# Three layers of edge convolution: comparison keys kept twice instead of four times, a fourth buffer for the compared keys, and count products in turns of three

## The chip, the cores and the metric

The kernel runs on one core of a Trainium2 chip. The metric is the device time of one execution in microseconds; three runs of the kernel before lie between 518.28 and 518.4 us. All times below are microseconds unless marked ns.

The engines are named as the profile names them: PE is TensorE (its matmuls), PEld the weight loads of TensorE, DVE VectorE, ACT ScalarE, POOL GpSimd, and SP the engine that issues most transfers.

## The reference

There are N = 2500 nodes with 256 features, and 80000 edges from `src` to `dst`, sorted by `dst`. A layer norm and a relu give h. Then come three layers and a final product over the concatenated results:

```python
def _edge_conv(x, src, dst, W, b):
    xi = x[dst]
    xj = x[src]
    m = jnp.concatenate([xi, xj - xi], axis=-1) @ W + b
    s = jax.ops.segment_sum(m, dst, num_segments=N)
    cnt = jax.ops.segment_sum(jnp.ones((dst.shape[0],), m.dtype), dst, num_segments=N)
    return s / jnp.maximum(cnt, 1.0)[:, None]

xs, h = [x], x                       # x: the normalized input
for W, b in ((W0, b0), (W1, b1), (W2, b2)):
    h = jax.nn.relu(_edge_conv(h, src, dst, W, b))
    xs.append(h)
return jnp.concatenate(xs, axis=-1) @ Wf + bf     # and the input is added
```

A layer is linear in the gathered features, so it can be done with a matrix A of counts: A[m, n] is how many edges go from node m to node n. Summing over edges then is a product with A, and the degrees are its column sums.

## The kernel before, in words

**Numbers.** Nodes are padded to NT = 20 tiles of 128. Six destination nodes (W = 6) make a window; there are 417 windows. For each window the kernel keeps a list of up to 256 edges (CH = 2 chunks of 128). Columns of A are worked in five groups (`GWS`: 84, 84, 84, 84 and 81 windows, that is 504 or 486 destination nodes).

**Keys.** For each edge there are two small numbers: the source node within its tile (0 to 127) in `key_m`, and tile and destination place (0 to 119) in `key_n`. `key_copy` (ACT, lines 579 to 584) writes them as bf16, each value four times in a row.

**Compare (DVE).** `compare(b)` (lines 753 to 767) takes four windows (BW = 4, eight chunks of 128 edges) and makes one-hot rows by two comparisons with running numbers: `one_m` (8 x 128 values) and `one_n` (8 x 120 values). The stored repeat makes the innermost piece of the key operand four adjacent values; the next step of that operand has stride 0, so the same four are read again for the whole row. The buffers of both are as many as `AHEAD`, 3.

**Count (PE).** `counts(b)` (lines 771 to 778) multiplies `one_m` by `one_n`, two bf16 products for each of the four windows, eight per call, into one PSUM bank. In the profile this is `bank<-one_n,one_m`.

**Take (ACT).** `take_counts(b, a)` casts a bank into the columns of the tile `a`, which holds A for one group. In the profile this is `a<-bank`.

**Aggregate (PE).** `layer(l, g, a, own)` (lines 816 to 838) adds up, over 20 tiles of source nodes, four products a tile: features in a high and a low part, `zh` and `zl`, times `a` (`pa<-a,zh` and `pa<-a,zl`). Four more units of work are the product with the node's own features (`pa<-hT,wt`); `own` says where in the sequence of 24 units they stand. It ends with a relu into `hT` on ACT.

**Stages.** The first 62 us prepare: edge lists are found, x is normalized, the first node products are made (`pz`), and the first group of A is counted. Their order over all engines is written out by hand in the string `order` (lines 863 to 872): Bn is `compare(n)`, Cn `counts(n)`, En `take_counts(n)`, and 21 calls of `compare` belong to a group. Then comes layer 0 (lines 899 to 927), group by group: while a group is aggregated, the next group's A is counted in between. `build` (lines 786 to 797) yields after each **turn**: two calls of `counts`, two of `take_counts`, two of `compare(c + AHEAD)`. The 21 calls of a group make 11 turns, the last with one call, and `at` (line 907) spreads them over the 24 units; the last stands after unit 22, with one unit to follow. All four engines keep to the program order in this stage (the class `InOrder`). `degrees` and `by_count` run beside it: the first makes the node degrees, with two small products (`bank<-ident_b,deg_b`), the second multiplies `hT` by them on DVE.

Layers 1 and 2 load finished groups of A back from HBM and count nothing. The banks for counts, degrees and node products are four in this stage (pool `ps`).

Of the kernel before, what the change touches and what calls it, by code (L numbers as in the profile page):

```python
# [11 lines left out]
OP = mybir.AluOpType  # L12
# [254 lines left out]
BF16 = mybir.dt.bfloat16  # L267
# [19 lines left out]
def run(it):  # L287
    for _ in it:
        pass
# [16 lines left out]
def chain(*its):  # L306
    for it in its:
        yield from it
# [3 lines left out]
def by_windows(ctx: ExitStack, tc: tile.TileContext, x, src, dst, Ws, bs, Wf, bf, out, missing):  # L312
# [3 lines left out]
    P = 128  # L316
# [9 lines left out]
    CH = 2  # L326
    S = 8
    CAP = CH * P
    NW = (N + W - 1) // W
# [1 line left out]
    WG = (NW + P - 1) // P  # L331
    NB = NT * W
    BW = 4
    AHEAD = 3
    GWS = []
    while sum(GWS) < NW:
        GWS.append(min(84, NW - sum(GWS)))
# [13 lines left out]
    const = ctx.enter_context(tc.tile_pool(name="const", bufs=1))  # L351
# [9 lines left out]
    def bank():  # L361
        return ps[-1].tile([P, 512], F32, name="bank")
# [3 lines left out]
    hT = const.tile([P, DC, NP], F32, name="hT")  # L366
    zh = const.tile([P, NT, D], F32R, name="zh")
    zl = const.tile([P, NT, D], F32R, name="zl")
    key_m = const.tile([P, NW, CH, 4], BF16, name="key_m")
    key_n = const.tile([P, NW, CH, 4], BF16, name="key_n")  # L370
    away = const.tile([P, WG, CAP], BF16, name="away")
    cnt = const.tile([P, NP], BF16, name="cnt")
    share = const.tile([P, NT], F32, name="share")
# [40 lines left out]
    ws = [None] * L  # L414
# [164 lines left out]
    def key_copy(i, q):  # L579
        n = min(P, NW - i * P)  # L580
        to = (key_m, key_n)[q]
        ACTo.copy(to[:, i * P:i * P + n, :, :].rearrange("p n j r -> p j n r"),
                  parts[i][:, q * CAP:(q + 1) * CAP].rearrange("p (j n) -> p j n", j=CH)[:, :, :n]
                  .unsqueeze(3).to_broadcast([P, CH, n, 4]))

    def degrees(i):

# [20 lines left out]
    def shares():  # L608
        cnt_n = bank()
        for t in range(NT):  # L610
            PEo.matmul(cnt_n[:, t:t + 1], cnt[0:1, t * P:(t + 1) * P], ones_b, start=True, stop=True)
        found = hot.tile([P, 1], F32, name="found")
        DVEo.reduce_sum(found, deg.rearrange("p i c -> p (i c)"), axis=mybir.AxisListType.X)
        pf = bank()
        PEo.matmul(pf[0:1, 0:1], found, ones, start=True, stop=True)
        DVEo.tensor_scalar(missing, pf[0:1, 0:1], float(E), None, op0=OP.not_equal)
        yield
        some = hot.tile([P, NT], F32, name="some")
        DVEo.tensor_scalar(share, cnt_n[:, :NT], 1.0, None, op0=OP.max)
        DVEo.reciprocal(share, share)  # L620
        DVEo.tensor_scalar(some, cnt_n[:, :NT], 1.0, None, op0=OP.min)
        DVEo.tensor_mul(share, share, some)
        yield
# [123 lines left out]
    def new_a(g):  # L747
        return apools[g % 2].tile([P, NT, GS], F32R, name="a")

    windows = [(g, s, min(BW, GWS[g] - s)) for g in range(NG) for s in range(0, GWS[g], BW)]  # L750
    ones_of = {}

    def compare(b):
        if b >= len(windows):
            return
        g, s, nb = windows[b]
        w0 = sum(GWS[:g]) + s
        one_m = hot.tile([P, BW * CH, P], BF16, name="one_m", bufs=AHEAD)
        one_n = hot.tile([P, BW * CH, NB], BF16, name="one_n", bufs=AHEAD)
        k = nb * CH  # L760
        for one, iota, keys_, m in ((one_m, iota_m, key_m, P), (one_n, iota_n, key_n, NB)):
            DVEo.tensor_tensor(
                one[:, :k, :].rearrange("p k (m r) -> p k m r", r=4),
                iota.rearrange("p (m r) -> p m r", r=4).unsqueeze(1).to_broadcast([P, k, m // 4, 4]),
                keys_[:, w0:w0 + nb, :, :].rearrange("p w j r -> p (w j) r").unsqueeze(2)
                .to_broadcast([P, k, m // 4, 4]), op=OP.is_equal)
        ones_of[b] = one_m, one_n

    counted = {}
# [1 line left out]
    def counts(b):  # L771
        _, s, nb = windows[b]
        one_m, one_n = ones_of.pop(b)
        pb = counted[b] = bank()
        for w in range(nb):
            for j in range(CH):
                PEo.matmul(pb[:, w * NB:(w + 1) * NB], one_m[:, w * CH + j, :], one_n[:, w * CH + j, :],
                           start=(j == 0), stop=(j == CH - 1))

    def take_counts(b, a):  # L780
        _, s, nb = windows[b]
        ACTo.copy(
            a[:, :, s * W:(s + nb) * W].rearrange("p t (w c) -> p t w c", c=W),
            counted.pop(b)[:, :nb * NB].rearrange("p (w t c) -> p t w c", w=nb, c=W))

    def build(g, a):

        bs = [b for b in range(len(windows)) if windows[b][0] == g]
        for b in bs[::2]:
            two = [b, b + 1] if b + 1 in bs else [b]  # L790
            for c in two:
                counts(c)
            for c in two:
                take_counts(c, a)
            for c in two:
                compare(c + AHEAD)
            yield

    def finish(g, a):
        c0, n = group_of(g)  # L800
        POOLo.tensor_copy(a[PAD:PAD + 1, NT - 1, :n], cnt[PAD:PAD + 1, c0:c0 + n])
        SP.dma_start(a_dram[g][:, :, :n], a[:, :, :n].bitcast(F32))
        yield
# [7 lines left out]
    def by_count(g):  # L811
        c0, n = group_of(g)
        for o in range(DC):
            DVEo.tensor_mul(hT[:, o, c0:c0 + n], hT[:, o, c0:c0 + n], cnt[:, c0:c0 + n])

    def layer(l, g, a, own, PE=PE, ACT=ACT):

        c0, n = group_of(g)
        pa = ps_agg.tile([P, DC, 512], F32, name="pa")
        ways = [(o, c) for o in range(DC) for c in range(DC)]  # L820
        units = [(0, k) for k in range(NT)]
        for i, u in enumerate(own):
            units.insert(u + i, (1, i))
        last = {}
        for kind, i in units:
            last.update({o: (kind, i, o) for o in (range(DC) if kind == 0 else ways[i][:1])})
        for kind, i in units:
            if kind == 0:
                for o in range(DC):
                    for z in (zh, zl):  # L830
                        PE.matmul(pa[:, o, :n], z[:, i, o * P:(o + 1) * P], a[:, i, :n],  # L831
                                  start=(i == 0 and z is zh), stop=(z is zl and last[o] == (kind, i, o)))
            else:
                o, c = ways[i]
                PE.matmul(pa[:, o, :n], ws[l][0][:, c, o * P:(o + 1) * P], hT[:, c, c0:c0 + n],  # L835
                          start=False, stop=(last[o] == (kind, i, o)))
            yield
        ACT.activation(hT[:, :, c0:c0 + n], pa[:, :, :n], AF.Relu)  # L838
# [8 lines left out]
    a = new_a(0)  # L847
# [4 lines left out]
        "se": lambda i: search(*((0, 1), (1, WG))[i]), "ge": get_edges,  # L852
        "ka": key_parts, "km": key_low, "kb": key_high, "kt": key_turn,
        "k1": lambda i: key_copy(i, 0), "k2": lambda i: key_copy(i, 1),
        "io": small_numbers, "ws": lambda: DVEo.tensor_sub(ws[0][0], ws[0][0], ws[0][1]),
        "st": stats, "rs": lambda g: spread(*groups[g]), "sq": lambda g: roots(*groups[g]),
# [11 lines left out]
        k11 N8 L6 B4 E2 L5 C3 B5 C4 T8 E3 E4 C5 V9 R8 E5 ge3 ka2 H9 sc2 Z7 H7 F8 G7 B6 N3 N2 ka3 km2 T2 R2 km3  # L868
        kb2 C6 T3 kb3 B7 L7 kt2 Z2 B8 B9 L9 E6 C7 k22 k12 kt3 H2 N4 E7 B10 k13 k23 Z8 L2 C8 T4 C9 E8 C10 H8 E9
        F9 B11 B12 C11 G8 E10 C12 R4 E12 E11 B13 F5 B14 C13 R3 B15 C14 E13 E14 L8 B16 Z3 G9 B17 C15 C16 H3 E15  # L870
        G5 B18 F3 C17 E16 C18 F4 E17 B19 C19 Z4 L3 G3 B20 E18 C20 B21 F2 E19 B22 E20 H4 L4 G4 B23 G2 ws
    """

    def perform(order):
# [24 lines left out]
    for g in range(NG):  # L899
        at = {}  # L900
        own = LATE
        if g + 1 < NG:
            a1 = new_a(g + 1)
            one = build(g + 1, a1)
            left = (len([b for b in windows if b[0] == g + 1]) + 1) // 2
            units = NT + DC * DC
            at = {(i + 1) * (units - 1) // left - 1 for i in range(left)}
            if g:
                own = [u + 1 - i for i, u in enumerate(sorted(at)[1:8:2])]
        else:  # L910
            extra = shares()
        for u, _ in enumerate(layer(0, g, a, own, PEo, ACTo)):
            if u in at:
                next(one)
            next(extra, None)
            if g == 0 and u % 2:
                next(extra, None)
            if g == 0 and u == NT // 2 + 3:
                by_count(0)
            if u == NT - 1 and g + 1 < NG:  # L920
                run(extra)
                by_count(g + 1)
        run(extra)
        if g + 1 < NG:
            run(finish(g + 1, a1))
            held, a = a, a1
        extra = chain(degrees(g + 2) if g + 2 < WG else ())
# [71 lines left out]
```

## Time and profile before

| | |
|---|---|
| median of three runs | 518.34 us (518.28 to 518.4) |
| the profiled execution | 518.31 us, of which the profiled span is 516.4 |
| PE busy | 509.2 us, 99% of the span |
| PEld busy | 405.9 us, 79% |
| DVE busy | 213.9 us, 41% |
| ACT busy | 138.4 us, 27% |
| granted PE clock | 0.999 |
| preparation | 0 to 61.7 us |
| layer 0, with four groups of A counted beside it | 61.7 to 211 us |

Busy time is added up per engine. A matmul's end is modelled and consecutive matmuls overlap, so a busy PE need not be a PE at full rate. What one matmul costs its successor is read from the difference of two starts in the timeline.

### The profile page before, as it was taken

What the parts mean: (1) busy time and instruction counts of PE and PEld (TensorE: products, weight loads), DVE (VectorE), ACT (ScalarE), POOL (GpSimd) and SP (SyncE); (2) the same over time, 40 slices, a digit from 0 to 9 for tenths busy, and PEclk for the clock granted to TensorE, in tenths of its full rate; (3) what the DMA queues carried; (4) which work ended last, traced back from release to release, by engine and by line L of the source; (5) the groups of instructions that cost most, each with busy time, mean ns of one, the idle gap of its engine ahead of it and who ended that gap; (6) DMA issues with size and microseconds to landing.
All of it is one profiled execution on the core that took longest, in us unless ns stands there. A gap on an engine that the chain in (4) does not pass through costs nothing.

```text
span 516.4 us, 6986 instructions
## 1 busy us (share of the span) xinstructions
PE 509.2 (99%) x2864; PEld 405.9 (79%) x2864; DVE 213.9 (41%) x455; ACT 138.4 (27%) x307; POOL 70.1 (14%) x103
## 2 busy tenths in 40 slices
PE   8999999999999999999999999999999999999996
PEld 4898888677777788788787878787887878787875
DVE  7999889887988840360101010103501010101033
ACT  5777576654643320330000000004300000000000
POOL 2680000000000000017242414200000000000000
PEclk9999999999999999999999999999999999999999
DMA  9110008950906428011576665100005564740023
GB/s 277 50 43 0 1 2 321 340 215 13 378 12 224 178 86 311 22 30 48 176 265 207 235 232 210 32 1 1 1 0 202 199 225 176 242 144 20 1 84 121
DMA packets 38111, 68.74 MB, mean 133 GB/s; under 512 B 1200, under 2 KB 37064, under 8 KB 38070
## 3 DMA queue, kind: packets, MB, share of 16 engines
q1 hardware_dynamic: 35798, 63.49, 34.9%
q0 software_dynamic: 1344, 3.61, 2.3%
q10 hardware_dynamic: 928, 1.11, 0.7%
q8 instruction: 24, 0.39, 0.3%
q14 instruction: 17, 0.14, 0.1%
HBM read 40.03 MB, written 28.18 MB: 132 GB/s over the span
## 4 chain that ended last, share of the span: by engine, by line
PE 96%; DMA 2%; DVE 0%; issue 0%; SPq 0%
PE pa L831 35%; PE pa L280 21%; PE bank L732 10%; PE bank L280 10%; PE bank L709 7%; PE pz L280 7%; PE pa L835 6%; DMA wf<-in_L_gnn_Wf_dram 2%; DMA dst_i<-in_dst_dram 1%; PE turned L280 1%; DVE acc L734 0%; DVE first L280 0%; SPq L280 0%
## 5 line engine op out<-in xcount | busy, mean ns | idle before, releaser
L831 PE MATMUL pa<-a,zh 128*128 128x504 f32 (+1 forms) x400 | 156.8, 392 | 0.0
L831 PE MATMUL pa<-a,zl 128*128 128x504 f32 (+1 forms) x400 | 155.0, 387 | 0.0
L734 DVE SCALAR_TENSOR_TENSOR acc<-bank,share,acc 128x256 f32<-128x256 f32 x60 | 29.0, 484 | 214.0 <-PE bank L732 214.0
L831 PEld LDWEIGHTS pa<-a,zl 128*128 128x128 f32 x400 | 75.2, 188 | 15.0
L831 PEld LDWEIGHTS pa<-a,zh 128*128 128x128 f32 x400 | 75.2, 188 | 15.0
L280 PE MATMUL pa<-a,zh 128*128 128x504 f32 (+1 forms) x200 | 84.7, 423 | 0.0
L280 DVE TENSOR_TENSOR one_m<-iota_m,key_m 128x1024 bf16<-128x1024 bf16 (+1 forms) x105 | 72.4, 690 | 15.4 <-PE bank L280 15.2
L280 PE MATMUL pa<-a,zl 128*128 128x504 f32 (+1 forms) x200 | 77.7, 388 | 0.0
L838 ACT ACTIVATE hT<-pa 128x1008 f32<-128x1008 f32 (+1 forms) x10 | 10.1, 1005 | 239.2 <-PE pa L835 239.2
L280 ACT CAST a<-bank 128x480 fp32r<-128x480 f32 (+1 forms) x105 | 54.5, 561 | 65.5 <-PE bank L280 62.7
L280 DVE TENSOR_TENSOR one_n<-iota_n,key_n 128x960 bf16<-128x960 bf16 (+1 forms) x105 | 68.3, 650 | 0.0
L280 PEld LDWEIGHTS <-one_m 128*128 128x128 bf16 x834 | 45.7, 98 | 13.5 <-DVE one_m L280 7.4
L280 PE MATMUL bank<-one_n,one_m 128*128 128x120 bf16 x834 | 53.9, 217 | 0.0
L732 PE MATMUL bank<-wf,hT 128*128 128x256 f32 x240 | 53.6, 379 | 0.0
L732 PEld LDWEIGHTS bank<-wf,hT 128*128 128x128 f32 x240 | 45.6, 190 | 9.9 <-issue 4.1
L280 PEld LDWEIGHTS pa<-a,zh 128*128 128x128 f32 x200 | 37.8, 189 | 9.0 <-issue 2.3
L280 PEld LDWEIGHTS pa<-a,zl 128*128 128x128 f32 x200 | 37.7, 188 | 8.1 <-issue 2.3
L719 DVE SCALAR_TENSOR_TENSOR zl<-bank,share,zh 128x256 fp32r<-128x256 f32 x38 | 18.4, 484 | 55.9 <-ACT zh L718 55.8
L835 PE MATMUL pa<-hT,wt 128*128 128x504 f32 (+1 forms) x80 | 35.2, 583 | 0.0
L709 PE MATMUL bank<-wb,hT 128*128 128x256 f32 x160 | 34.9, 379 | 0.0
L709 PEld LDWEIGHTS bank<-wb,hT 128*128 128x128 f32 x160 | 30.4, 190 | 4.9 <-issue 0.9
L835 PEld LDWEIGHTS pa<-hT,wt 128*128 128x128 f32 x80 | 15.2, 190 | 14.6 <-issue 13.8
(113 smaller groups left out, 337.9 us busy)
## 6 DMA issues: line engine op xcount, KB each, us to landing
a<-a_dram SPq DMA_DIRECT2D x5, 5040.0 KB, 17.3
a_dram<-a SPq DMA_DIRECT2D x4, 5040.0 KB, 17.2
a_dram<-a SPq DMA_DIRECT2D x1, 4860.0 KB, 17.1
a<-a_dram SPq DMA_DIRECT2D x1, 4860.0 KB, 16.6
zf<-in_x_dram POOLq DMA_DIRECT2D x19, 128.0 KB, 3.1
out_dram<-acc SPq DMA_DIRECT2D x19, 128.0 KB, 1.7
wf<-in_L_gnn_Wf_dram SPq DMA_DIRECT2D x4, 256.0 KB, 9.1
acc<-in_x_dram SPq DMA_DIRECT2D x1, 896.0 KB, 10.0
```

Source lines behind the costliest of these rows:

```text
L280: return self.tc.keep_in_program_order(call(*args, **kwargs))
L709: PE.matmul(pz[:, :D], hT[:, c, t * P:(t + 1) * P], ws[l][1][:, c, :], start=(c == 0), stop=(c == DC - 1))
L719: DVE.scalar_tensor_tensor(zl[:, t, :], pz[:, :D], sc, zh[:, t, :].bitcast(F32), op0=OP.mult, op1=OP.subtract)
L732: PE.matmul(po[:, :D], hT[:, c, t * P:(t + 1) * P], wfs[l][:, c, :], start=(c == 0), stop=(c == DC - 1))
L734: DVE.scalar_tensor_tensor(acc[:, t, :], po[:, :D], share[:, t:t + 1], acc[:, t, :], op0=OP.mult, op1=OP.add)
L831: PE.matmul(pa[:, o, :n], z[:, i, o * P:(o + 1) * P], a[:, i, :n], start=(i == 0 and z is zh), stop=(z is zl and last[o] == (kind, i, o)))
L835: PE.matmul(pa[:, o, :n], ws[l][0][:, c, o * P:(o + 1) * P], hT[:, c, c0:c0 + n], start=False, stop=(last[o] == (kind, i, o)))
L838: ACT.activation(hT[:, :, c0:c0 + n], pa[:, :, :n], AF.Relu)
```

## The change

The repeat of the keys goes from four to two (`REP`), which halves `key_m` and `key_n`; the comparisons read two adjacent values again and again instead of four. `AHEAD` goes from 3 to 4, so `one_m` and `one_n` have four buffers each, and `compare` runs one call further ahead; `B24` joins the written order. A turn of `build` has three calls instead of two (`TURN`): 21 calls make 7 turns. The turns stand after the units 2, 5, 8, 12, 15, 18 and 22 (before: 1, 3, 5 and so on to 19, and 22), and the four own units of groups 1 to 4 follow the turns after the old units 5, 8, 12 and 15.

```diff
@@ -331,7 +331,9 @@
     BW = 4
-    AHEAD = 3
+    TURN = 3
+    REP = 2
+    AHEAD = 4
@@ -366,8 +368,8 @@
-    key_m = const.tile([P, NW, CH, 4], BF16, name="key_m")
-    key_n = const.tile([P, NW, CH, 4], BF16, name="key_n")
+    key_m = const.tile([P, NW, CH, REP], BF16, name="key_m")
+    key_n = const.tile([P, NW, CH, REP], BF16, name="key_n")
@@ -581,7 +583,7 @@
         to = (key_m, key_n)[q]
         ACTo.copy(to[:, i * P:i * P + n, :, :].rearrange("p n j r -> p j n r"),
                   parts[i][:, q * CAP:(q + 1) * CAP].rearrange("p (j n) -> p j n", j=CH)[:, :, :n]
-                  .unsqueeze(3).to_broadcast([P, CH, n, 4]))
+                  .unsqueeze(3).to_broadcast([P, CH, n, REP]))
@@ -760,10 +762,10 @@
             DVEo.tensor_tensor(
-                one[:, :k, :].rearrange("p k (m r) -> p k m r", r=4),
-                iota.rearrange("p (m r) -> p m r", r=4).unsqueeze(1).to_broadcast([P, k, m // 4, 4]),
+                one[:, :k, :].rearrange("p k (m r) -> p k m r", r=REP),
+                iota.rearrange("p (m r) -> p m r", r=REP).unsqueeze(1).to_broadcast([P, k, m // REP, REP]),
                 keys_[:, w0:w0 + nb, :, :].rearrange("p w j r -> p (w j) r").unsqueeze(2)
-                .to_broadcast([P, k, m // 4, 4]), op=OP.is_equal)
+                .to_broadcast([P, k, m // REP, REP]), op=OP.is_equal)
@@ -786,14 +788,13 @@
         bs = [b for b in range(len(windows)) if windows[b][0] == g]
-        for b in bs[::2]:
-            two = [b, b + 1] if b + 1 in bs else [b]
-            for c in two:
-                counts(c)
-            for c in two:
-                take_counts(c, a)
-            for c in two:
-                compare(c + AHEAD)
+        for i in range(0, len(bs), TURN):
+            for b in bs[i:i + TURN]:
+                counts(b)
+            for b in bs[i:i + TURN]:
+                take_counts(b, a)
+            for b in bs[i:i + TURN]:
+                compare(b + AHEAD)
             yield
@@ -868,7 +869,7 @@
-        G5 B18 F3 C17 E16 C18 F4 E17 B19 C19 Z4 L3 G3 B20 E18 C20 B21 F2 E19 B22 E20 H4 L4 G4 B23 G2 ws
+        G5 B18 F3 C17 E16 C18 F4 E17 B19 C19 Z4 L3 G3 B20 E18 C20 B21 F2 E19 B22 E20 H4 L4 G4 B23 B24 G2 ws
@@ -902,11 +903,11 @@
-            left = (len([b for b in windows if b[0] == g + 1]) + 1) // 2
+            left = -(-len([b for b in windows if b[0] == g + 1]) // TURN)
             units = NT + DC * DC
             at = {(i + 1) * (units - 1) // left - 1 for i in range(left)}
             if g:
-                own = [u + 1 - i for i, u in enumerate(sorted(at)[1:8:2])]
+                own = [u + 1 - i for i, u in enumerate(sorted(at)[1:5])]
```

## The prediction

> **What bounds the kernel now.** I read the page's busy times first, then its slices, then the sums of two stretches, the waits, and last the timeline around one turn.
>
> ```profile
> PE 509.2 (99%) x2864; PEld 405.9 (79%) x2864; DVE 213.9 (41%) x455; ACT 138.4 (27%) x307; POOL 70.1 (14%) x103
> ...
> DVE  7999889887988840360101010103501010101033
> ```
>
> PE is never idle for long, so a gain has to come from fewer PE instructions or from their spacing. The DVE row shows two programs: nearly full to the fourteenth slice (180 us), nearly empty after. The change touches only the full part. The sums of busy time over the preparation from 20 us on and over layer 0 (stretch; PE, PEld, DVE, ACT, POOL; clock) say how full:
>
> ```profile
> 20.00:61.68 41.68, 41.68 (x341) 37.19 (x339) 39.59 (x83) 30.08 (x59) 16.66 (x16) 1.00 0.07 20
> 61.68:190.01 128.33, 128.33 (x1067) 99.13 (x1065) 107.41 (x189) 65.92 (x161) 5.18 (x6) 1.00 0.47 169
> ```
>
> DVE is the second bound: 39.59 of 41.68 us in the preparation, 107.41 of 128.33 in layer 0. The waits say who waits for whom there (total, times, longest):
>
> ```profile
> DVE one_m L280 <- PE bank L280: 15.2, 31, 2.0
> ...
> PEld L280 <- DVE one_m L280: 7.4, 28, 0.3
> ```
>
> The comparisons wait 15.2 us for PE to free buffers, which is their slack. The other line looks like PE waiting for comparisons, but it is a weight load of at most 0.3 us each time, the same length as waits that other turns put down to "issue"; the timeline shows that it delays no matmul:
>
> ```profile
> 83.16 0.39 PE L280 MATMUL pa<-a,zh 128*128 128x504 f32 x1
> 83.16 0.19 PEld L280 LDWEIGHTS pa<-a,zl 128*128 128x128 f32 x1
> ...
> 83.39 0.39 PE L280 MATMUL pa<-a,zl 128*128 128x504 f32 x1
> ...
> 83.62 0.85 PEld L280 LDWEIGHTS <-one_m 128*128 128x128 bf16 x16 [0.27 <-DVE one_m L280]
> 83.62 1.02 PE L280 MATMUL bank<-one_n,one_m 128*128 128x120 bf16 x16
> ...
> 84.42 0.19 PEld L280 LDWEIGHTS pa<-a,zh 128*128 128x128 f32 x1
> 84.45 0.47 PE L280 MATMUL pa<-a,zh 128*128 128x504 f32 x1
> 84.53 0.19 PEld L280 LDWEIGHTS pa<-a,zl 128*128 128x128 f32 x1
> 84.76 0.39 PE L280 MATMUL pa<-a,zl 128*128 128x504 f32 x1
> ```
>
> From start to start: pa to pa 0.23 (83.16 to 83.39), the last pa to the counts also 0.23, sixteen counts 0.83 (0.052 each). But the first pa after the counts takes 0.31 (84.45 to 84.76). Its weight load starts 0.03 before it, while inside a run the load starts a whole matmul ahead. So **each return from counts costs about 0.08 us**. The last turn of group 1, with only eight counts, pays the same: first pa at 125.54, the next at 125.86. So it is a price per turn, not per count. A turn followed by an own unit pays it too: 104.53 to 107.20 is 2.67, against 16 x 0.052 + 2 x 0.424 + 4 x 0.2275 = 2.59.
>
> [...] starts 0.60 and 0.57 apart. [...]
>
> ```profile
> L280 DVE TENSOR_TENSOR one_m<-iota_m,key_m 128x1024 bf16<-128x1024 bf16 x104 | 72.2, 694 | 15.4 <-PE bank L280 15.2
> ...
> L280 DVE TENSOR_TENSOR one_n<-iota_n,key_n 128x960 bf16<-128x960 bf16 x104 | 68.0, 654 | 0.0
> ...
> L280 ACT CAST a<-bank 128x480 fp32r<-128x480 f32 x104 | 54.2, 564 | 63.2 <-PE bank L280 60.4 <-issue 2.8
> ```
>
> **The change part by part.**
>
> 1. *Turns of three.* Four groups are counted beside layer 0: 44 turns become 28. The counts themselves stay. Saved: 16 x 0.083 = **1.33 us**, all on PE, the bounding engine. The written order of PE's instructions confirms 24 counts where 16 stood, and that own units still stand right behind a turn.
>
> 2. *Degree products.* Six small matmuls that stand alone between pa runs cost the same return. Two places change, one to each side; I count **+0.02** for the twelve in group 0, which now follow four pa and not the counts. The degrees are computed on DVE, in group 0 behind the comparisons of the turn after unit 5: these start 0.6 after the turn, last 3 x 1.17 = 3.5, and the degrees 0.6 more, 4.7 together. PE asks for them after 24 counts, 12 pa and 24 counts, 1.25 + 2.82 + 1.25 = 5.3. In groups 1 and 2 an own unit adds 0.85 to that. Covered; without the cover, at most 0.5 us each.
>
> 3. *The last turn of a group.* The next group's first pa needs all columns of its A. Before, the last turn had eight counts: PE then had one unit to do while ACT cast one bank. In the page's time at 93.22: counts start, cast 93.83 to 94.39, pa at 94.45. Now there are 24 counts (1.25 us) and three casts. The first cast starts 0.63 after the counts (83.62, 84.25), two take 1.02, so three end near 0.63 + 1.53 = 2.16, plus some 0.05 to be seen. PE arrives at 1.25 + 0.85 = 2.10 behind group 0 (own unit last) and 1.25 + 0.91 + 0.08 = 2.24 in groups 1 to 3. So a **new wait of about 0.1 us** once, and none to 0.15 at the other three, if the weight load cannot go ahead. I take +0.15 in all, with 0 to 0.6 for the range. Queued behind those casts on ACT is the group's relu into `hT`, needed only by work a unit of layer later; behind the last column on POOL is one row copy and on SP the 17 us store, which must be over before the buffer's next use about 30 us later.
>
> 4. *Banks.* Three count banks and up to two degree banks rotate over four. ACT empties one in 0.51; a turn comes every 4.4 us. A degree product right behind a turn takes the fourth bank, the next the first again, which is cast by 1.2 us after the turn began; its counts last 1.25. Taken as nothing. No run shows a shortage, so up to 0.3 us a group for the range.
>
> 5. *Fourth buffer, B24.* B24 adds 1.17 us to DVE at the end of the preparation, before `ws`, which is needed at unit 20 of group 0, over 20 us later. Its compare needs a buffer that count 20 frees at 60.1. In a turn DVE has 3 x 1.17 = 3.5 us of work in 4.4 and one compared call in stock. Nothing on the path. That the new buffers move the tiles behind them in memory I cost at nothing, as spacing does not show addresses.
>
> 6. *Keys twice.* Six casts of 1.02 us on ACT write half as much; the cast of 512 values into `zh` takes 0.59, so ACT gets some 2.5 us back in the preparation. PE is gapless there and DVE takes its keys well ahead; no gain. The comparisons keep their 1.17 us a pair [...]. I take 0; the bound above is 1.02 more a pair.
>
> Sum: -1.33 + 0.02 + 0.15 = -1.16. From the profiled 518.31, which is 516.4 of span plus 1.9 around it, that gives 517.15; against the median 518.34, as near the same, **517.1 us**.
>
> **Rivals.**
>
> *Slower: the comparisons [...].* [...] Price: call 20 is counted at 59.66 and its comparison ended at 57.84, so the preparation has 1.8 us of slack over 21 calls; 21 x 1.02 - 1.8 = 20 us. In layer 0 a group would need 21 x 2.19 + 1.8 = 48 us of DVE against 31 of PE: some 60 us over the four groups. Time: about **597 us**. The point from which it decides is low: more than 0.09 us a pair (8%) uses up the preparation's slack; above 1.39 a pair DVE bounds layer 0 too.
>
> *No difference: the saving is eaten.* The waits of step 3 reach 0.15 at all four ends, and degree products or banks wait once. For it: ACT's margin there is under 0.1 us by my sum. Against: it needs nearly all the upper ends. Time: 517.4 to 518.3, about **517.8**.
>
> *The saving is not per turn.* If a scheduler split the turns, or if the return cost grew with the counts in front of it, nothing is won: 518.3. The written order excludes the first; eight, sixteen and two counts with the same 0.08 to 0.09 speak against the second.
>
> **How the numbers follow.** What a measurement of this kernel can tell from no change is about 0.2%, 1.04 us, so my forecast stands just beyond that edge. I give the forecast as worked out, up to 517.3, 0.54; the eaten saving in its two forms, up to 518.9 with some small waits more, 0.28; the slow comparison, whole or in part, 0.15, and other losses 0.03. The range starts at 516.6 (no wait at all is 517.0; a return of 0.1 instead of 0.083 takes 0.27 more) and ends at 518.9, leaving out the slow comparison.
>
> **What would show it.** Right: `one_m` still near 690 ns; 24 counts in 1.25 us and then one pa of 0.31; starts of layer 1's node products near 209.8 instead of 211.0. Step 3: the waits show PEld at `pa<-a` waiting for ACT at group ends. Wrong: `one_m` over 1 us, weight loads of counts waiting for DVE over 1 us each, PE gaps in the slices before 61 us.

## The result, and the profile after

The changed kernel takes **517.2 us** (median of 11 runs, 516.78 to 517.51); the kernel before takes 518.28 (11 runs, 518.01 to 518.77). The ratio is 0.9977, with a 95% interval of 0.9969 to 0.9985: about 1.1 us faster. The profiled execution took 517.24 us, of which 515.4 is the span, 1.0 less than before.

The page after, busy times and the DVE row of the slices (tenths):

```profile
PE 508.1 (99%) x2864; PEld 407.2 (79%) x2864; DVE 213.5 (41%) x455; ACT 134.1 (26%) x307; POOL 68.5 (13%) x103
...
DVE  7989998889888840360101010103501010101033
```

PE has as many instructions as before and is busy 1.1 us less. ACT has 4.3 us less work. The stretches of the prediction, the second ending 1 us earlier here, show where ACT lost most of it (stretch, with its length; then PE, PEld, DVE, ACT, POOL; clock, DMA share, GB/s):

```profile
20.00:61.68 41.68, 41.42 (x336) 36.69 (x335) 39.08 (x83) 26.91 (x59) 15.86 (x16) 1.00 0.08 20
61.68:189.00 127.32, 127.32 (x1067) 100.82 (x1066) 107.55 (x189) 64.25 (x161) 3.80 (x6) 1.00 0.47 171
```

In the preparation ACT goes from 30.08 to 26.91: the key casts write half. But PE, gapless in the kernel before (41.68 of 41.68), now has 0.26 us of gaps.

The groups of the comparisons (count; busy, mean ns; idle before) answer the question whether repeat two costs DVE anything:

```profile
L280 DVE TENSOR_TENSOR one_m<-iota_m,key_m 128x1024 bf16<-128x1024 bf16 x104 | 71.8, 691 | 15.2 <-PE bank L280 15.1
...
L280 DVE TENSOR_TENSOR one_n<-iota_n,key_n 128x960 bf16<-128x960 bf16 x104 | 69.4, 667 | 0.0
```

They stand at 691 and 667 ns, where 694 and 654 stood. In the timeline a pair of them still takes 1.17 us from start to start (84.12 to 85.29), as before. The waits (total, times, longest) show a slack of DVE that did not move, and a wait of PE's weight loads for ACT that had been there once, for 0.6 us, and is now there four times:

```profile
DVE one_m L280 <- PE bank L280: 15.1, 23, 2.1
...
PEld pa L280 <- ACT a L280: 1.2, 4, 0.6
```

One turn of group 0 in the timeline (start, length):

```profile
82.84 1.44 PE L280 MATMUL bank<-one_n,one_m 128*128 128x120 bf16 x24
...
84.09 0.48 PE L280 MATMUL pa<-a,zh 128*128 128x504 f32 x1
...
84.41 0.39 PE L280 MATMUL pa<-a,zl 128*128 128x504 f32 x1
...
84.64 0.39 PE L280 MATMUL pa<-a,zh 128*128 128x504 f32 x1
```

Start to start: 24 counts in 1.25 us, the first pa in 0.32, the next in 0.23. The return costs about as much behind 24 counts as behind 16 (0.09 here, 0.08 in the prediction's turn).

To see where the microsecond came from I split every span at two marks: the first pa product (end of the preparation) and the first node product of layer 1 (end of layer 0). What lies behind the second mark is called the rest; no instruction of the rest was edited. The marks, for the kernel before and then for the changed kernel:

```profile
61.68 0.58 PE L280 MATMUL pa<-a,zh 128*128 128x504 f32 x1
...
210.88 3.40 PE L709 MATMUL bank<-wb,hT 128*128 128x256 f32 x15
```

```profile
61.98 0.58 PE L280 MATMUL pa<-a,zh 128*128 128x504 f32 x1
...
210.36 3.83 PE L711 MATMUL bank<-wb,hT 128*128 128x256 f32 x17
```

| kernel | preparation | layer 0 | rest | span |
|---|---|---|---|---|
| before | 61.68 | 149.20 | 305.52 | 516.4 |
| after | 61.98 | 148.38 | 305.04 | 515.4 |
| difference | +0.30 | -0.82 | -0.48 | -1.0 |

Spans are given to 0.1 us, so a rest is good to about 0.05. Each row is one execution.

So the sum came out as forecast, but its parts did not: layer 0 gave 0.82 and not 1.16, the preparation got longer, and the rest, where I expected nothing, gave almost half of the total. The experiments had to say which of these belongs to which edit.

### The profile page after: what moved, and what is told of

Same layout as the page of the kernel before. It is cut to its first block, busy times and chain, and to the rows that moved or that the text cites. A ratio compares the mean times of both kernels' runs of the same rounds, so it can differ in the third digit from the quotient of the medians.

```text
span 515.4 us, 6981 instructions
## 1 busy us (share of the span) xinstructions
PE 508.1 (99%) x2864; PEld 407.2 (79%) x2864; DVE 213.5 (41%) x455; ACT 134.1 (26%) x307; POOL 68.5 (13%) x103
## 3 DMA queue, kind: packets, MB, share of 16 engines
q10 hardware_dynamic: 928, 1.11, 0.7%
## 4 chain that ended last, share of the span: by engine, by line
PE 90%; DVE 4%; DMA 3%; POOL 2%; issue 1%; SPq 0%; DVEq 0%
PE pa L832 35%; PE pa L280 21%; PE bank L734 10%; PE bank L280 8%; PE bank L711 7%; PE pa L836 7%; PE pz L280 2%; DMA acc<-in_x_dram 2%; POOL acc L280 1%; DVE one_m L280 1%; DVE st L280 1%; DMA es<-in_src_dram,start_i 1%; POOL ed L280 1%; DVE one_n L280 1%; POOL es L280 0%
## 5 line engine op out<-in xcount | busy, mean ns | idle before, releaser
L280 ACT CAST a<-bank 128x480 fp32r<-128x480 f32 (+1 forms) x105 | 52.9, 565 | 68.5 <-PE bank L280 65.9
L280 DVE TENSOR_TENSOR one_n<-iota_n,key_n 128x960 bf16<-128x960 bf16 (+1 forms) x105 | 69.7, 664 | 0.0
L280 PE MATMUL bank<-one_n,one_m 128*128 128x120 bf16 x834 | 51.4, 217 | 0.3
```

Of the source, the lines that this page charges most:

```text
L280: return self.tc.keep_in_program_order(call(*args, **kwargs))
```

## The experiments

Each ratio is to the kernel before on the same chip, with its 95% interval.

### The turns alone: kernel before with turns of three

```diff
+    TURN = 3
-        for b in bs[::2]:
+        for i in range(0, len(bs), TURN):
...
-                own = [u + 1 - i for i, u in enumerate(sorted(at)[1:8:2])]
+                own = [u + 1 - i for i, u in enumerate(sorted(at)[1:5])]
```

The repeat stays four, the buffers three, and B24 stays out.

> The kernel before with turns of three alone: keys four times, three buffers, no B24. If the turns bring the gain, layer 0 takes about 145.1 us as in the changed kernel, and the whole is 0.8 to 1.1 us faster than before. With three buffers no call is in stock after a turn, so the third comparison of a turn has next to no slack: by the durations it is ready when PE comes, within 0.1 us, so up to 0.1 a turn may be lost, 2.8 us at most. If the fourth buffer is what makes turns of three possible, that loss shows as weight loads of counts waiting for DVE, and the gain is gone. If addresses do it, layers 1 and 2 take the time of before.

Measured: 517.12 us, ratio 0.9978 (0.9972 to 0.9985). Its two marks:

```profile
61.47 0.58 PE L280 MATMUL pa<-a,zh 128*128 128x504 f32 x1
...
209.56 4.70 PE L711 MATMUL bank<-wb,hT 128*128 128x256 f32 x21
```

The preparation ends at 61.47, layer 0 takes 148.09, the rest 305.54. **The turns alone bring as much as the whole change**, and they bring it in layer 0: 1.11 us less than before, where steps 1 to 3 summed to 1.16. The preparation, 0.21 shorter in this execution, was not edited. Three buffers are enough for turns of three.

### Everything but the turns: changed kernel with turns of two

```diff
-    TURN = 3
+    TURN = 2
...
-                own = [u + 1 - i for i, u in enumerate(sorted(at)[1:5])]
+                own = [u + 1 - i for i, u in enumerate(sorted(at)[1:8:2])]
```

> The changed kernel with turns of two again (44 turns); keys twice, four buffers and B24 stay, own units stand as before the change. If the turns bring the gain, layer 0 (first pa product to the last group's own units) takes 145.9 us again instead of 145.1, and the whole is 0.8 us or more slower than the changed kernel, near 518.0 to 518.3. If the fourth buffer or the halved keys bring it, it stays near 517.2 and layer 0 near 145.1. It also says whether layers 1 and 2, 0.5 us shorter in the changed kernel's profile, stay so with the tiles where the change put them: if the addresses do it, they do.

Measured: 517.83, ratio 0.9990 (0.9981 to 0.9998). Layer 0 takes 149.32, as in the kernel before within 0.12. The rest takes 304.87, which is 0.65 less than before: the gain sits where this kernel and the kernel before run the same instructions.

### The keys alone: kernel before with repeat two

```diff
-    key_m = const.tile([P, NW, CH, 4], BF16, name="key_m")
-    key_n = const.tile([P, NW, CH, 4], BF16, name="key_n")
+    key_m = const.tile([P, NW, CH, REP], BF16, name="key_m")
+    key_n = const.tile([P, NW, CH, REP], BF16, name="key_n")
```

and the casts and patterns of the comparison likewise, with REP = 2; turns of two, three buffers.

> The kernel before with only the keys halved (repeat 2): turns of two, three buffers each, no B24. If step 6 holds, the comparisons keep 690 and 655 to 670 ns and the casts in the preparation get about 3 us shorter in sum, with nothing won: 518.3 us. Layer 0 then is 149.2 us as in the kernel before, since turns are as many. What can move is the rest, if the place of A in memory (6672 bytes lower here) sets the pace of the last passes: 0 to 0.65 us less there, so 517.6 to 518.3. A layer 0 below 149.0 would mean that the halved keys themselves help PE, against my reading that only the number of turns does.

Measured: 518.44, ratio 1.0005 (0.9996 to 1.0013). Comparisons at 691 and 659 ns; ACT in the preparation 27.16; layer 0 149.19; rest 305.51. Halving the keys does nothing to the time. The rest did not move either, so of the parts of the previous experiment it is the fourth buffers with B24, or where they put the other tiles, that go with the 0.65 us. And not every move of a tile matters: with the shorter keys alone, A lies 6656 bytes a partition lower than in the kernel before (3328 for each key tile; the expectation's 6672 is 16 too many), and its passes take the same time (20.27, 17.69 and 17.68 us for the group of 486 columns). No run has the fourth buffers beside keys of four.

### The price of a turn from the other side: turns of one

```diff
+    TURN = 1
...
+                own = [u + 1 - i for i, u in enumerate([sorted(at)[k] for k in (3, 7, 10, 14)])]
```

on the kernel before: 84 turns instead of 44.

> The kernel before with turns of one: 84 turns instead of 44, own units kept near their old places. Where an own unit stands alone between two turns there is no return to pa, so some 30 returns are added. At 0.083 to 0.09 us each that is 2.5 to 2.7 us more, near 521.0. If the price grew with the number of counts ahead of the return, eight counts would cost half of sixteen and the time would stay near 518.3 to 518.8.

Measured: 521.16, ratio 1.0056 (1.0041 to 1.0071). Layer 0 takes 151.99, which is 2.79 more than before for 40 turns more: 0.070 a turn. The last turns of the groups have eight counts in both kernels. Not every turn has a switch of its own at both ends, since own units and degree products stand next to some. Counted in PE's order, layer 0 changes from one kind of product to another (aggregate, count, degree, own) 112 times before and 179 times here. That is 33.5 more changes away and back, at 0.083 each, the price that the prediction read from a single turn.

### Turns of four, and of five

```diff
-    TURN = 3
+    TURN = 4
```

on the changed kernel: 24 turns, the last of a group with one call.

> The changed kernel with turns of four: six turns a group, 24 instead of 28, and the last of a group has a single call. If the price is per return, 4 x 0.09 = 0.35 us less, and 0.2 less because the last turn has one cast again; layer 0 near 147.9 instead of 148.4, the whole near 516.7. Against it: with four buffers all four comparisons of a turn (4.7 us) must be done between two turns some 5.2 us apart, and all four banks are in use, so a degree product right behind a turn must wait for the first cast. If that decides, weight loads of counts wait for DVE, and the time is 517.2 or more.

Measured: **516.36**, ratio 0.9963 (0.9949 to 0.9976), the shortest of all kernels here. All its five runs (516.32 to 516.54) lie below all runs of the changed kernel with the last turn earlier (516.63 to 517.61, median 517.01) and with the pad (516.67 to 517.47, median 517.11), both further down, on the same chip; the changed kernel itself has no runs beside these. Layer 0 takes 147.92, 0.46 less than after. The last-turn wait of step 3 is down from four times to one, since a last turn of one call leaves ACT one cast. The rest takes 304.85.

```diff
-    TURN = 3
+    TURN = 5
...
-    AHEAD = 4
+    AHEAD = 5
```

on the changed kernel, with B25 in the order, and with three small tiles (`junk2`, `some`, `found`) kept in one buffer and the unused tile `between` gone: 20 turns.

> Turns of five: five turns a group, 20 instead of 28, the last with one call; five buffers for the compared keys (AHEAD 5, B25 added), for which three small tiles give up their second buffer and an unused gap of 96 bytes goes. A turn needs five of the four banks, but the first bank's cast ends 1.2 us after the turn began and the fifth count starts at 1.66. If the price is per return, 0.6 us less than turns of four: layer 0 near 147.3 us, the whole near 515.8. If banks or comparisons (five, 5.85 us, in about 6.2) run out, weight loads of counts wait for ACT or DVE and it is 516.4 or more. The addresses of A change again, which may add or take up to 0.5 us.

Measured: 517.8, ratio 0.9989 (0.9982 to 0.9996). Layer 0 falls again, to 147.55. But the rest grew to 306.54, 1.5 us above after. In the rest a pass is the run of 80 products of A with `zh` and `zl` that aggregates one group in one layer. The chain of that kernel (start, length, products) shows one of the passes that grew, with the same pass of the changed kernel in the second fence:

```profile
255.62 18.32 PE pa L831 x80
```

```profile
256.41 18.15 PE pa L832 x80
```

All eight passes of 504 columns take 18.31 or 18.32 us instead of 18.15, which is 1.3 us in all, and the last one of 486 columns takes 17.60 instead of 17.34. They are the same 80 products a pass; what differs is where the tiles lie, and what ran before them. Which of the two did it was not tried on this kernel. Turns of five gain in the stage that they change and lose more in one that they don't.

### The tiles moved back: a pad

```diff
     const.tile([P, 24], F32, name="between")
+    const.tile([P, 672], F32, name="apart")
```

The unused tile puts A at the addresses that it had in the kernel before; weights and compared keys, which also lie behind it, move by the same 2688 bytes. The features `zh` and `zl` stay where they were in all kernels.

> The changed kernel with an unused tile of 2688 bytes a partition ahead of the tiles that hold A, so that these, and all behind them, lie at the addresses of the kernel before. In layers 1 and 2 the changed kernel's two passes over the 486-column group take 17.60 and 17.34 us where the kernel before takes 17.69 and 17.68, with nothing in the code of these layers changed. If the addresses of A do it, both passes take 17.7 again and the part from the first node product on takes 305.5 us instead of 305.0; the whole is about 0.4 us slower, near 517.6. If it is something else, both stay.

Measured: 517.11, ratio 0.9977 (0.9968 to 0.9986), as the changed kernel without the pad. Inside, two things swapped: layer 0 fell to 148.05, that of the turns alone (148.09), and the rest rose to 305.25. In layer 0 it is the pace of A's products: 262 of 504 columns that stand among their like in groups 0 to 3 took 59.95 us from start to start in the changed kernel, 59.74 with the pad and 59.72 with the turns alone. The last pass of 486 columns in the chain, for the pad, after and before in turn:

```profile
472.45 17.68 PE pa L833 x80
```

```profile
472.70 17.34 PE pa L832 x80
```

```profile
473.31 17.68 PE pa L831 x80
```

For this pass the pad brings back exactly the time of before. For the first 486-column pass it doesn't: that takes 17.69 before, 17.60 after, 17.59 with the pad. So moving the tiles by 2688 bytes, with nothing else changed, moved this pass by 0.34 us and layer 0 by 0.33, in opposite directions, and on the total the pad's two effects cancelled.

### One value at a time: repeat one

```diff
-    REP = 2
+    REP = 1
```

> The changed kernel with each key kept once, so that the innermost piece of the key operand is one value read again and again. This is the slow case of the prediction made real: [...] one_m takes about 1.13 us from start to start instead of 0.60 and one_n 1.06, DVE bounds the preparation (some 20 us more) and layer 0 (some 60 us more), and the whole is near 597 us. [...] the time stays at 517.2. In between: the preparation alone, about 537.

Measured: 602.8, ratio 1.163 (1.1609 to 1.1652), at a granted PE clock of 0.972. The groups (count; busy, mean ns; idle before):

```profile
L280 POOL CAST a<-cnt 1x504 fp32r<-1x504 bf16 (+1 forms) x5 | 105.6, 21127 | 118.1 <-issue 75.0
...
L280 DVE TENSOR_TENSOR one_m<-iota_m,key_m 128x1024 bf16<-128x1024 bf16 (+1 forms) x105 | 127.5, 1214 | 0.0
...
L280 DVE TENSOR_TENSOR one_n<-iota_n,key_n 128x960 bf16<-128x960 bf16 (+1 forms) x105 | 120.6, 1149 | 0.0
```

The comparisons nearly double, and DVE never idles before them. Starts in the timeline are 1.13 and 1.07 apart, against 1.13 and 1.06 expected: 1.03 more a pair than the 1.17 of repeat four and two, where the prediction's bound has 1.02. The slow rival is thus real, but it needs repeat one (1222 and 1156 ns without the short last call); with repeat two the comparisons took 691 and 667. Why one value at a time is slower, no run shows. The preparation ends at 80.47 (18.8 later than before, worked out as 20), and layer 0 takes 215.1 (66 longer). The prediction writes some 60 for layer 0, but that is a slip: its own 48 against 31 us a group is 17, over four groups 68.

### The last turn one place earlier

```diff
-            at = {(i + 1) * (units - 1) // left - 1 for i in range(left)}
+            at = {(i + 1) * (units - 2) // left - 1 for i in range(left)}
```

on the changed kernel.

> The changed kernel with the seven turns of a group after units 2, 5, 8, 11, 14, 17 and 21: the last one has two units behind it instead of one, and own units follow the turns as before. If the three casts after the last turn hold PE up at the group's end, those waits go: the weight load at pa no longer waits for ACT, and layer 0 is 0.1 to 0.2 us shorter than the 148.4 of the changed kernel (from its first pa product to the first node product of layer 1). The whole may then be 517.0; 517.2 if there is no such wait.

Measured: 517.01, ratio 0.9977 (0.9967 to 0.9988). The wait of PEld at `pa<-a` for ACT is gone from the list, layer 0 takes 148.30, 0.08 less. The own units and degree products have shifted with the turns, so the 0.08 is not the price of the waits alone. The wait of step 3 is real and small.

### Two attempts on the preparation

In the changed kernel, DVE stands still once in the preparation, for the last edge list; behind it PE's counts take 0.3 us too long, twice. The DVE and the POOL timeline (start, length; in brackets the wait before it):

```profile
36.10 0.40 DVE L280 TENSOR_SCALAR lo_i<-es 128x256 int32<-128x256 int32 x1 [1.16 <-DMA es<-in_src_dram,start_i]
```

```profile
23.27 3.31 POOL L280 TENSOR_SCALAR acc<-acc,rs,off 128x256 f32<-128x256 f32 x2
...
33.87 4.55 POOL L280 TENSOR_SCALAR acc<-acc,rs,off 128x256 f32<-128x256 f32 x6 [0.24 <-DVE off L280]
```

POOL fetches the lists, and two normalizations stand in its queue ahead of the later fetches. They took 3.31 us here and 2.38 in the kernel before, where DVE's wait was 0.67:

```profile
35.84 0.36 DVE L280 TENSOR_SCALAR lo_i<-es 128x256 int32<-128x256 int32 x1 [0.67 <-DMA es<-in_src_dram,start_i]
```

```profile
23.21 2.38 POOL L280 TENSOR_SCALAR acc<-acc,rs,off 128x256 f32<-128x256 f32 x2
...
34.10 5.73 POOL L280 TENSOR_SCALAR acc<-acc,rs,off 128x256 f32<-128x256 f32 x6 [0.92 <-DVE off L280]
```

First I moved a comparison into the wait:

```diff
-        k11 N8 L6 B4 E2 ... H7 F8 G7 B6 N3 N2 ka3 km2 T2 R2 km3
-        kb2 C6 T3 kb3 B7 L7 kt2 ...
+        k11 N8 L6 B4 E2 ... H7 F8 G7 B6 B7 N3 N2 ka3 km2 T2 R2 km3
+        kb2 C6 T3 kb3 L7 kt2 ...
```

> The changed kernel with B7 written ahead of ka3 (after B6) instead of behind kb3; the fourth buffer lets it run there. In the changed kernel's profile DVE waits 1.16 us before ka3 for the last edge list and PE then stands twice for 0.3 us at counts, and layer 0 starts at 61.98 us. If that wait sets the end of the preparation, the comparison fills it, the two stalls go and layer 0 starts near 61.4, the whole is 0.3 to 0.6 us faster than the changed kernel, near 516.7. If PE alone sets it, the start stays near 61.9 and the time at 517.2.

Measured: 517.59, ratio 0.9986 (0.9979 to 0.9992); layer 0 starts at 62.28, later than in the changed kernel, and the median is 0.48 above that of the pad on the same chip. A miss. The POOL and the PEld timeline say why:

```profile
33.61 6.23 POOL L280 TENSOR_SCALAR acc<-acc,rs,off 128x256 f32<-128x256 f32 x6 [0.24 <-DVE off L280]
```

```profile
38.15 0.20 PEld L280 LDWEIGHTS turned<-shift,acc 128*128 128x128 f32 x2 [0.61 <-POOL acc L280]
```

DVE's gap was filled, and then POOL's six normalizations took 6.23 us instead of 4.55, and PE waited for POOL. Second, on the kernel with turns of four, I gave the two normalizations (N9) to ACT, somewhat earlier in the order:

```diff
-            if q >= 2:
+            if q >= 2 and q != Q - 1:
...
-        rs2 Z6 ge1 L1 T7 B0 R5 R7 Z5 B1 C0 B2 ka1 G6 H6 N9 H5 C1
+        rs2 Z6 ge1 L1 T7 B0 R5 N9 R7 Z5 B1 C0 B2 ka1 G6 H6 H5 C1
```

> Turns of four, and the normalization of the last two node tiles (N9) on ACT, where it idles 1.35 us, instead of on POOL, between two fetches of edge lists. In the profiles these two POOL operations take 2.4 or 3.3 us beside DVE's comparisons, 0.84 each elsewhere, and all later edge fetches wait behind them. If the arrival of the last edge list sets the end of the preparation, DVE no longer waits for it, PE has no stall at counts, and layer 0 starts at 61.3 us or before instead of 61.5 to 62.2, the whole near 515.9 instead of 516.4. If PE alone sets the end, the start stays near 61.8 and the time at 516.4; if ACT then delays the turned tiles, it is later.

Measured: 516.88, ratio 0.9969 (0.9956 to 0.9981), where turns of four without this edit had 516.36 on another chip; layer 0 starts at 62.26 instead of 61.83. A miss in the same way: the lists come in time, DVE goes on without a break, and POOL's six take longer still.

```profile
33.34 7.25 POOL L280 TENSOR_SCALAR acc<-acc,rs,off 128x256 f32<-128x256 f32 x6 [3.80 <-DVE off L280]
```

## Why the prediction came out, point by point

**Step 1, turns of three: right.** With nothing else changed they take 1.11 us off layer 0, and that is net of the last-turn waits. The price a return that I read from one timeline, 0.083, holds up: in turns of one, 33.5 more changes of product away and back cost 2.79 (0.083 each). Turns of three have 81 changes where 112 stood, 15.5 fewer away and back, and gained 1.11 net of the 0.2 of step 3: 0.084 each. Turns of four (77 changes) and five (65) gain another 0.46 and 0.37, but those are not pure, since waits and pass times differ beside the turns.

**Step 2, degree products: about right over the layer, too small in group 0.** I counted +0.02. In group 0 the returns to A's products fell from ten to seven, so four turns fewer saved only three, and about 0.08 was lost there; the later groups made most of it good. Over layer 0, 16 turns fewer are 32 changes fewer, and 31 were found, which is about 0.04.

**Step 3, the last turn: right.** The waits show it as the prediction said, four times, while it had been there once. Longest 0.6, but that is the weight load's idle time; what PE loses is seen in the own unit ahead of it, 0.89 us from start to start where 0.81 stood, and 0.03 to 0.05 at the other three ends: 0.2 in all, forecast 0.15.

**Step 4, banks: right.** No wait for a bank arose in layer 0.

**Step 5, fourth buffer: the step that failed.** DVE's part is as said: B24 is hidden. What failed is "That the new buffers move the tiles behind them in memory I cost at nothing". What went with the new buffers was worth -0.48 us in the rest and about +0.29 in layer 0 (148.38 against 148.09 for the turns alone). That the place in memory does it is shown by the pad for layer 0 and for the last pass. It is not the whole account, though. The passes over the 486-column group, read from the chains (layer 0's last: its last 76 products with A, and eight own ones):

| kernels | layer 0's last pass | first 486 pass | last 486 pass |
|---|---|---|---|
| three buffers: before, turns alone, turns of one, keys alone | 20.27 | 17.69 | 17.68 |
| four buffers, turns of two or four | 20.18 | 17.34 | 17.34 |
| four buffers, turns of three | 20.34 | 17.60 (17.59) | 17.34 |

The second and the third row have the same tiles at the same places, and differ only in the size of a turn. The first 486 pass in the chain, for turns of four and for after:

```profile
231.50 17.34 PE pa L832 x80
```

```profile
232.10 17.60 PE pa L832 x80
```

(The third row is after, the last turn earlier, and the comparison moved forward; the second row includes the one with N9 on ACT. The pad and turns of five place the tiles otherwise and stand in no row.) So the odd turn goes with something that I have not found. In the first row neither the size of a turn (one, two or three) nor A's place (6656 bytes lower for the keys alone) makes a difference. Half of the 0.84 us that turns of four gain over the change lies in these passes, 0.16 in layer 0's last and 0.26 in the first of 486 columns. The other half fits, roughly, two changes of product away and back fewer (0.17), the last-turn waits of step 3 (0.2) and a preparation that was 0.15 shorter in the profiled execution.

**Step 6, keys twice: right in its sum, wrong in a premise.** Alone they change nothing (1.0005), and ACT gets 2.9 us back in the stretch from 20 to 61.68 (30.08 to 27.16, forecast 2.5). `one_m` took 691 ns with an innermost count of two, 694 with four and 1222 with one. But "PE is gapless there" holds only for the execution that I had. In after, sixteen counts took 1.13 and 1.15 us from start to start, twice, where 0.84 is their pace. It is not the halved keys: turns of one on the kernel before, with keys of four, show the same 3.31 us on POOL and end the preparation at 61.89, and the turns alone show 2.36 and 61.47. In nine kernels whose written order there is the same but for B24 the preparation ended at 61.47 to 62.20, one execution each; what decides within that is open, and the 0.30 of after lies inside it.

**The rivals.** The slow comparison did not come, but no trace of the kernel before excluded it: that two adjacent values are as quick as four is shown only by the result (a pair in 1.17 us). Nor did a trace show its price. Repeat one did: 1.03 us more a pair where the prediction set 1.02, and 602.8 where it had 597, or 605 with the slip in layer 0 put right (68 instead of 60). The saving was not eaten, and it did not depend on the counts in front of a return: a product with A right behind counts started its successor 0.31 to 0.32 us later, on average, behind eight, sixteen, 24 or 32 of them, and 0.23 later among its like.

**The sum.** -1.16 forecast, -1.11 for the turns alone; with the measured terms -1.33 + 0.04 + 0.2 = -1.09. That the whole change lands at the same figure is partly luck: -0.48 in the rest, +0.29 in layer 0 and +0.30 in the preparation, none of which I had in the sum, add to +0.1. One sign shows it: layer 1's node products were to start near 209.8 and start at 210.36, while with the turns alone they start at 209.56.

## What to carry to other kernels

Where PE bounds and alternates between two kinds of product, count the switches and read the price of one from two starts in the timeline (0.08 us here). Turns of three instead of two took 1.11 us off layer 0 here, net of some 0.2 us for which emptying the banks of the last turn held up the next group. So choose the turn so that the last one is short: with turns of four, whose last has one call, one of four such waits was left. (It does not do it alone: turns of five, with the same last call, show four again, 1.9 us in all for the weight loads.) When a change moves tiles in memory, compare by stage: stages that were not edited moved by half a microsecond here, and by 1.5 with turns of five, which can hide or fake the effect of a small edit. And a gap that is filled on one engine can come with a slower neighbour (POOL's six normalizations took 4.55 us beside DVE's gap and 6.23 without it): before filling it, look at how long the neighbour's instructions take with the gap and without.

## What the runs showed of the hardware that I had not expected

**POOL was slower where DVE did not pause.** Six normalizations on POOL took 4.55 us where DVE had stood 1.16 us, 5.73 in the kernel before where it had stood 0.67, and 6.23 and 7.25 where it went on. With comparisons of 1.2 us back to back, three of the four casts of 504 values in one row took 29 to 46 us and one took 0.9, where the four took 1.0 on average in the kernel before. Why POOL is slower then, the runs do not show. Layer 0 of the kernel with repeat one took 66 us more, against 68 from DVE's work alone, so nothing shows that the long casts, or the clock of 0.972, cost time there.

**The same product at another address.** 80 products of 486 columns took 17.34, 17.60 or 17.68 us, and 80 of 504 columns 18.15, 18.13 or 18.32, at a granted clock of about 1.00. The spread is up to 2%, and repeats: the kernels of one row of the table above agree pass by pass. Within a pass the pace is even: in the changed kernel nearly all products of the first 486-column pass start 220 ns apart, and those of the last 216 or 217. That an address is part of it is shown by the pad. By which rule an address is good or bad stays open: A moved by 2688 bytes with an effect (17.34 against 17.68 for the last pass) and by 6656 without one (17.68 in both), and two moves don't make a rule. What the size of the turn has to do with it stays open too.
